# Half of the output projection's passes taken among the query products of the chunk ahead

## The chip, the cores and the metric

The kernel runs on one core of a Trainium2 chip. The metric is the time of one execution on the device in microseconds (us), of which lower is better. A core has five engines with a queue of instructions each, worked off in order: TensorE (PE in the profile; its weight loads are a row of their own, PEld), VectorE (DVE), ScalarE (ACT), GpSimd (POOL) and SyncE (SP), which here only issues DMA transfers. Engines wait for each other by semaphores.

## What is computed

One transformer layer on x of 2 x 1024 tokens x 512, all in f32: `x = x + layernorm(attention(layernorm(x)))`, then `x = x + layernorm(ffn(layernorm(x)))`. What matters here is the attention with its output projection, cut to its core:

```python
q = hidden_states @ Wq      # 32 heads of 128
k = hidden_states @ Wk      # 8 key heads, each for 4 query heads
v = hidden_states @ Wv
gs = log_sigmoid(k) / 16
o_lin = gla_scan(softmax(q), softmax(k), v, gs)      # S = S * exp(g_t) + k_t v_t;  o_t = q_t S
y = sliding_window_attn(rope(q), rope(k), v)         # window of 64
o_ = (0.5 * y + 0.5 * o_lin).astype(bfloat16).astype(float32)
o = o_ @ Wo                                          # 4096 -> 512
```

The feed-forward part first rounds its three weight matrices to 16 levels per block of 64 (NF4), and then computes `w3(silu(w1 x) * (w2 x))`.

## The kernel before, in words

The attention is `fast_attention`. Its main loop (`for n in range(N_)`, line 769) runs over 128 chunks in the order of key head g (8), batch b (2) and block of 128 tokens c (8). A chunk is the work of 128 tokens and the 4 query heads of one key head. Keys are made for two chunks at once, so even and odd iterations differ: an even one holds the key products of the next pair (`key_products`, line 412), an odd one holds the gates and the key transposes of that pair.

The loop is software-pipelined by hand. In iteration n the scores, the two attention parts and the values of chunk n are computed, the queries of chunk n + 1 are prepared, and the output of chunk n - 1 is projected. All engines are wrapped so that instructions keep the order in which the program writes them (`InOrder`, line 110; `product` is TensorE's matmul and records line 117, as every wrapped operation does). So the order on each engine is the order of calls in the loop body. On TensorE an odd iteration is:

- `scores(n)` (tile ps)
- `query_products(n + 1)` (tile pq): the 128 tokens times Wq for 4 heads, four products of 128x512 over the 512 inputs (kt = 0 to 3), two passes each in f32
- `key_gates` (pg), `linear(n)` (pa, and ot from the state S), `mix(n)` (softmaxed scores sw transposed into pa)
- `project(n - 1)` (tile py)
- `key_transposes` (pt, pg), `rope_transposes(n + 1)` (tr), `values(n)` (ot from A), `softmax_transposes(n + 1)` (tq), `state_products(n)` (pS)

In an even iteration `linear` follows the query products directly, then come `key_products` (pk) and `mix`, then `project`, `rope_transposes`, `softmax_transposes`, `values`.

What follows pq on the other engines: ScalarE copies it to q (line 509), GpSimd rotates q into qr by four operations (`rope`, line 377: qtmp, two halves of qr, their sum), and TensorE transposes qr (line 528), from which ScalarE copies qrT for the next scores. VectorE takes pq's maxima (nmq), ScalarE its exponentials in place, VectorE divides (qs), and TensorE transposes qs (tq).

What follows pk in even iterations: ScalarE copies it to kv, VectorE takes maxima (nmk), ScalarE makes gate and ke.

`project` (line 623) multiplies the rounded heads oc of chunk n - 1, 128x128 for each of 4 heads, by the head's rows of Wo. These stand in the tile wop as two parts, a rounded one and its remainder (i = 0, 1), both of type F32R; a product of F32R is one pass. So there are eight passes of 128x512 that add into one PSUM bank, py. The tile oc comes from ob by ScalarE: `heads(n)` scales ot into ob (bf16) at the end of iteration n, and `rounded_heads(n)` casts it to oc early in iteration n + 1. `collect` (line 631) adds py to yacc on VectorE. The tiles ot and py alternate in a pool of two PSUM banks (line 313), pq, pk and pg in another of two.

Between these calls, `signs` and `steps` place pieces of the weight rounding for the feed-forward part on ScalarE (zs, zp, zm) and VectorE. At the end of each key head the next Wo rows are split into wop by GpSimd (`part_weights`). The last 16 iterations also begin the feed-forward part.

Of the kernel before, what the change touches and what calls it, by code (L numbers as in the profile page):

```python
# [11 lines left out]
F32 = mybir.dt.float32  # L12
# [9 lines left out]
P = 128  # L22
NB, N, HID = 2, 1024, 512
H, KVH, D, W = 32, 8, 128, 64
GRP = H // KVH
# [95 lines left out]
def sandwich_kernel(ctx: ExitStack, tc: tile.TileContext, x, wq, wk, wv, wo, w1, w2, w3, out, con):  # L121
# [154 lines left out]
    def load_out_weights(g):  # L276
        nc.sync.dma_start(wos, wo[g * GRP * D : (g + 1) * GRP * D, :].rearrange("(h p) d -> p h d", p=P))
        return wos
# [20 lines left out]
    def fast_attention():  # L299

        with ExitStack() as attn:
# [11 lines left out]
            po = attn.enter_context(tc.tile_pool(name="fpo", bufs=2, space=PSUM))  # L313
# [3 lines left out]
            product = tensor.matmul  # L317
# [5 lines left out]
            def parts_tile(name):  # L323
                return wop.tile([P, 2, GRP, HID], F32R, tag="wop", name=name)
# [43 lines left out]
            weights = {0: (*first_weights, parts_tile("wop0"), load_out_weights(0))}  # L368
# [8 lines left out]
            def rope(dst, tmp, src, c, nch, heads):  # L377

                shape = [P, nch, heads, D]
                hd = D // 2  # L380
                cs = cosT[:, c : c + nch, :].unsqueeze(2).to_broadcast(shape)
                sn = sinT[:, c : c + nch, :].unsqueeze(2)
                gpsimd.tensor_tensor(tmp, src, cs, ALU.mult)
                half = [P, nch, heads, hd]
                gpsimd.tensor_tensor(dst[:, :, :, 0:hd], src[:, :, :, hd:D], sn[:, :, :, 0:hd].to_broadcast(half), ALU.mult)
                gpsimd.tensor_tensor(dst[:, :, :, hd:D], src[:, :, :, 0:hd], sn[:, :, :, hd:D].to_broadcast(half), ALU.mult)
                gpsimd.tensor_tensor(dst, dst, tmp, ALU.add)
# [20 lines left out]
            chunks = [(g, b, c) for g in range(KVH) for b in range(NB) for c in range(NCH)]  # L408
            N_ = len(chunks)
            keys, Q, S = {}, {}, {}  # L410
# [87 lines left out]
                gpsimd.memset(eq[:, :, W : W + 1], 1.0)  # L498
                K.update(krT=krT, khT=khT, khz=khz, eq=eq, em=em, before=None)

            def query_products(n):

                g, b, c = chunks[n]
                ci = b * NCH + c
                pq = pmm.tile([P, GRP, D], F32, tag="mm", name="pq")
                for kt in range(KT):
                    product(pq.rearrange("p h d -> p (h d)"), lhsT=xnT[:, kt, ci * P : (ci + 1) * P], rhs=weights[g][0][:, kt, :], start=kt == 0, stop=kt == KT - 1)
                q = q1p.tile([P, GRP, D], F32, tag="q", name="q")
                scalar.copy(q, pq)
                qr = q1p.tile([P, GRP, D], F32, tag="qr", name="qr")  # L510
                tmp = q1p.tile([P, GRP, D], F32, tag="qtmp", name="qtmp")
                rope(qr.unsqueeze(1), tmp.unsqueeze(1), q.unsqueeze(1), c, 1, GRP)
                Q[n] = {"pq": pq, "qr": qr}
# [55 lines left out]
            def score_masks(n):  # L569
                sc = Q[n]["sc"]  # L570
                vector.tensor_tensor(sc, sc, fwin[:, 1 if chunks[n][2] == 0 else 0], ALU.add)
                Q[n]["nms"] = row_max(sc, 4, "s")

            def score_exps(n):
                Q[n]["sms"] = row_exps(Q[n]["sc"], Q[n]["sc"], Q[n]["nms"], 4, "s")
# [42 lines left out]
            def rounded_heads(n):  # L618
                oc = q2p.tile([P, GRP, P], F32R, tag="oc", name="oc", bufs=1)
                scalar.copy(oc, Q[n]["ob"])  # L620
                Q[n]["oc"] = oc

            def project(n):
                g, oc, parts = chunks[n][0], Q[n]["oc"], weights[chunks[n][0]][2]
                py = po.tile([P, HID], F32, tag="o", name="py")
                for h in range(GRP):
                    for i in range(2):
                        product(py, lhsT=oc[:, h, :], rhs=parts[:, i, h, :], start=h == 0 and i == 0, stop=h == GRP - 1 and i == 1)
                Q[n]["py"] = py

            def collect(n):

# [136 lines left out]
            for n in range(N_):  # L769
                g, b, c = chunks[n]  # L770

                inputs = [AHEAD + n] if AHEAD + n < NCI else []
                even = n % CB == 0
                more, keys2 = n + 1 < N_, n + CB < N_


                scores(n)
                if n:
                    rounded_heads(n - 1)
                score_masks(n)  # L780
                query_decays(n)
                if n:
                    next_state(n - 1)
                if n == N_ - 2:
                    F.token_sums(0, vector)
                signs(2 if even else 1, n)
                steps(1, n)
                score_exps(n)
                if more:
                    query_products(n + 1)  # L790
                if even:
                    query_max(n + 1)
                    query_exps(n + 1)
                    signs(3, n)
                    score_softmax(n)
                    steps(1, n)
                    linear(n)
                    if keys2:
                        key_products(n + CB)
                    else:  # L800
                        first = F.hidden(0, 0, ("gate", "gate", "tr", "tr"))
                        next(first)
                    query_softmax(n + 1)
                    steps(1, n)
                    for ci in inputs:
                        input_norms(ci)
                        input_measured(ci + 1)
                    feed_forward_tokens(n)
                    if keys2:
                        key_softmax(n + CB)  # L810
                    mix(n)
                    steps(1, n)
                    if keys2:
                        key_sums(n + CB)
                    if n:
                        project(n - 1)
                        collect(n - 1)
                    if not keys2:
                        next(first)
                    rope_transposes(n + 1)  # L820
                    softmax_transposes(n + 1)
                    signs(1, n)
                    values(n)
                    heads(n)
                    steps(2, n)
                    if n == 0:
                        for h in range(2, GRP):
                            part_weights(0, h)
                else:
                    if not more:  # L830
                        for i in range(4):
                            next(first)
                    score_softmax(n)
                    if not more:
                        next(first)
                        next(first)
                        list(F.weight_sums(1))
                    if more:
                        query_max(n + 1)
                        key_gates(n + 1)  # L840
                        query_exps(n + 1)
                        key_decays(n + 1)
                    signs(2, n)
                    linear(n)
                    mix(n)
                    if more:
                        query_softmax(n + 1)
                    project(n - 1)
                    collect(n - 1)
                    for ci in inputs:  # L850
                        input_norms(ci)
                        input_measured(ci + 1)
                    feed_forward_tokens(n)
                    if more:
                        key_transposes(n + 1)
                        rope_transposes(n + 1)
                    else:
                        second = F.hidden(0, 1, ("gate", "gate", "up", "tr"))
                        for i in range(4):
                            next(second)  # L860
                    values(n)
                    if more:
                        softmax_transposes(n + 1)
                    heads(n)
                    steps(2, n)
                state_products(n)
                for ci in inputs:
                    input_transposes(ci)
                feed_forward_begun(n)
                if b == 1 and c == 0 and g + 1 < KVH:  # L870
                    weights[g + 1] = all_weights(g + 1)
                if b == 1 and NCH - GRP <= c and g + 1 < KVH:
                    part_weights(g + 1, c - NCH + GRP)
            rounded_heads(N_ - 1)
            for i in range(4):
                next(second)
            project(N_ - 1)
            collect(N_ - 1)
            list(F.weight_sums(2))

# [670 lines left out]
```

## Time and profile before

| | |
|---|---|
| median of 3 runs | 2108.78 us (2108.52 to 2109.44) |
| the profiled execution | 2109.49 us, of which the span from first to last instruction is 2107.6 us |
| granted TensorE clock, mean | 0.998 |
| DMA | 64.65 MB, 31 GB/s in the mean |

The profile's page lists, for each engine, busy time and its share of the span. Then it has rows of one form: line, engine, operation, output tile <- input tiles, sizes, count; behind the first bar are busy time and mean ns of one; behind the second the idle time of the engine before them and who ended it. A matmul's record contains the time until its results are drained, which overlaps the next matmul, so that spacing and duration differ. The timeline gives instructions in order of time: start in us, length in us (of several merged ones together), engine, line, operation, tiles, count, and in brackets the idle time before and who ended it. The chain that ended last is followed back from the end; its rows give start and length of each piece. The attention's loop fills the time from some 30 us to 1660 us; behind it stands the rest of the feed-forward part.

### The profile page before, as it was taken

What the parts mean: (1) busy time and instruction counts of PE and PEld (TensorE: products, weight loads), DVE (VectorE), ACT (ScalarE), POOL (GpSimd) and SP (SyncE); (2) the same over time, 40 slices, a digit from 0 to 9 for tenths busy, and PEclk for the clock granted to TensorE, in tenths of its full rate; (3) what the DMA queues carried; (4) which work ended last, traced back from release to release, by engine and by line L of the source; (5) the groups of instructions that cost most, each with busy time, mean ns of one, the idle gap of its engine ahead of it and who ended that gap; (6) DMA issues with size and microseconds to landing.
All of it is one profiled execution on the core that took longest, in us unless ns stands there. A gap on an engine that the chain in (4) does not pass through costs nothing.

```text
span 2107.6 us, 29467 instructions
## 1 busy us (share of the span) xinstructions
PE 2067.5 (98%) x9476; PEld 1503.0 (71%) x9476; DVE 1593.1 (76%) x3123; ACT 1394.4 (66%) x4045; POOL 1125.8 (53%) x1524
## 2 busy tenths in 40 slices
PE   7999999999999999999999999999999999999998
PEld 4767777777777777777777777777767785858583
DVE  4888888888888888888888888788886663838352
ACT  4777888888888888888888888888876440202010
POOL 5555755565566556554655574556554452627250
PEclk9999999999999999999999999999999999999999
DMA  6100100010011001000100010000011030000000
GB/s 226 36 11 20 57 16 11 21 51 10 11 36 40 11 16 41 31 11 11 50 21 10 26 57 12 11 17 22 16 36 35 26 102 21 21 20 16 21 1 22
DMA packets 48307, 64.65 MB, mean 31 GB/s; under 512 B 6736, under 2 KB 22736, under 8 KB 48144
## 3 DMA queue, kind: packets, MB, share of 16 engines
q1 hardware_dynamic: 48144, 62.68, 9.4%
q8 instruction: 77, 1.26, 0.2%
q14 instruction: 86, 0.70, 0.1%
HBM read 50.01 MB, written 12.65 MB: 30 GB/s over the span
## 4 chain that ended last, share of the span: by engine, by line
PE 82%; DVE 7%; ACT 6%; POOL 3%; issue 1%; DMA 0%; ACTq 0%; POOLq 0%; DVEq 0%
PE pq L117 17%; PE pout L117 12%; PE py L117 9%; PE pk L117 8%; PE ot L117 8%; PE pa L117 6%; PE ps L117 5%; PE pup L117 3%; PE pgate L117 3%; PE tr L117 3%; PE tq L117 2%; ACT ps L117 2%; PE pg L117 2%; POOL qr L117 1%; ACT pq L117 1%
## 5 line engine op out<-in xcount | busy, mean ns | idle before, releaser
L117 POOL TENSOR_TENSOR qtmp<-q,tables 128x512 f32<-128x512 f32 x128 | 162.5, 1270 | 568.4 <-ACT q L117 564.0
L117 PE MATMUL pq<-wq,xnT 128*128 128x512 f32 x1024 | 460.7, 592 | 1.6 <-ACT xnT L117 1.6
L117 PEld LDWEIGHTS pq<-wq,xnT 128*128 128x128 f32 x1024 | 184.8, 190 | 185.4 <-issue 185.4
L117 ACT ACTIVATE zs<-xw,fbounds 128x512 bf16<-128x512 f32 (+3 forms) x416 | 287.9, 723 | 0.0
L117 PE MATMUL py<-wop,oc 128*128 128x512 f32 x1024 | 270.8, 406 | 0.0
L117 ACT ACTIVATE ps<-ps,nms 128x128 f32<-128x128 f32 x512 | 175.1, 342 | 111.4 <-DVE nms L117 96.9
L117 ACT ACTIVATE pq<-pq,nmq 128x128 f32<-128x128 f32 x512 | 175.2, 342 | 91.7 <-DVE nmq L117 79.3
L117 PE MATMUL pk<-wkv,xnT 128*128 128x256 f32 x1024 | 231.5, 379 | 0.0
L117 PEld LDWEIGHTS pk<-wkv,xnT 128*128 128x128 f32 x1024 | 194.5, 190 | 46.5 <-issue 16.3
L117 PEld LDWEIGHTS py<-wop,oc 128*128 128x128 f32 x1024 | 182.9, 189 | 35.0
L117 POOL TENSOR_TENSOR qr<-q,tables 128x256 f32<-128x256 f32 x256 | 206.6, 828 | 0.0
L117 DVE SCALAR_TENSOR_TENSOR zp<-zp,zs 128x512 f32<-128x512 f32 (+3 forms) x224 | 196.9, 879 | 9.2 <-ACT zs L117 4.7
L117 POOL TENSOR_TENSOR qr<-qr,qtmp 128x512 f32<-128x512 f32 x128 | 165.8, 1295 | 10.1
L117 DVE SCALAR_TENSOR_TENSOR zm<-zm,zs 128x512 f32<-128x512 f32 (+3 forms) x192 | 163.6, 852 | 5.3 <-ACT zs L117 2.9
L117 DVE TENSOR_TENSOR ps<-ps,fwin 128x512 f32<-128x512 f32 x128 | 89.2, 697 | 101.9 <-PE ps L117 101.2
L117 PE MATMUL ps<-kT,qrT 128*128 128x128 f32 x1024 | 136.7, 277 | 2.8 <-POOL kT L117 2.6
L117 DVE TENSOR_REDUCE nmq<-pq 128x4 f32<-128x512 f32 x128 | 87.8, 686 | 62.2 <-ACT q L117 61.2
L117 POOL TENSOR_TENSOR rstd<-ve,mhalf 128x1 f32<-128x1 f32 x62 | 36.5, 588 | 172.3 <-DVE ve L117 172.2
L117 PEld LDWEIGHTS ps<-kT,qrT 128*128 128x128 f32 x1024 | 124.8, 192 | 5.0 <-POOL kT L117 4.0
L117 PE MATMUL ot<-qh,S 128*128 128x512 f32 x224 | 114.4, 592 | 0.0
L117 POOL COPY vm<-kv 64x128 f32<-64x128 f32 (+1 forms) x176 | 99.6, 581 | 3.1
L117 ACT ACTIVATION_READ_ACCUMULATOR pq<-pq,nmq 128x1 f32 x512 | 98.8, 193 | 0.0
(311 smaller groups left out, 4587.0 us busy)
## 6 DMA issues: line engine op xcount, KB each, us to landing
wq<-in_L_attn_Wq_dram SPq DMA_DIRECT2D x8, 1024.0 KB, 5.6
wos<-in_L_attn_Wo_dram SPq DMA_DIRECT2D x8, 1024.0 KB, 5.4
wq<-_attn_hidden_states_dram SPq DMA_DIRECT2D x20, 256.0 KB, 2.8
xw<-in_L_ffn_w_dram SPq DMA_DIRECT2D x20, 256.0 KB, 2.6
dq<-zp SPq DMA_DIRECT2D x20, 256.0 KB, 2.0
wos<-dq SPq DMA_DIRECT2D x20, 256.0 KB, 2.7
out_dram<-ffoc SPq DMA_DIRECT2D x16, 256.0 KB, 2.0
tokens<-_attn_hidden_states_dram SPq DMA_DIRECT2D x12, 256.0 KB, 5.4
```

Source lines behind the costliest of these rows:

```text
L117: return lambda *args, **kwargs: self.tc.keep_in_program_order(getattr(self.engine, name)(*args, **kwargs))
```

## The change

In every iteration but the first, the four passes of `project(n - 1)` with part i = 0 are called from within `query_products(n + 1)`, one behind each of its four products. The four with i = 1 stay at the place of the former call. The eight products and what they add up to are the same; their order goes from head outermost to part outermost. The tile py is opened with the first of them. In the last iteration, which has no query ahead, the first four are called where the query products would be, and the projection of the last chunk makes both calls one after the other. `skip_group_check` is an argument for the program's builder and no instruction.

```diff
-            def query_products(n):
+            def query_products(n, done=None):
...
                 for kt in range(KT):
                     product(pq.rearrange("p h d -> p (h d)"), lhsT=xnT[:, kt, ci * P : (ci + 1) * P], rhs=weights[g][0][:, kt, :], start=kt == 0, stop=kt == KT - 1)
+                    if done is not None:
+                        project(done, 0, [kt])
...
-            def project(n):
-                g, oc, parts = chunks[n][0], Q[n]["oc"], weights[chunks[n][0]][2]
-                py = po.tile([P, HID], F32, tag="o", name="py")
-                for h in range(GRP):
-                    for i in range(2):
-                        product(py, lhsT=oc[:, h, :], rhs=parts[:, i, h, :], start=h == 0 and i == 0, stop=h == GRP - 1 and i == 1)
-                Q[n]["py"] = py
+            def project(n, i, heads=range(GRP)):
+
+                oc, parts = Q[n]["oc"], weights[chunks[n][0]][2]
+                if "py" not in Q[n]:
+                    Q[n]["py"] = po.tile([P, HID], F32, tag="o", name="py")
+                for h in heads:
+                    product(Q[n]["py"], lhsT=oc[:, h, :], rhs=parts[:, i, h, :], start=i == 0 and h == 0, stop=i == 1 and h == GRP - 1, skip_group_check=True)
...
                 if more:
-                    query_products(n + 1)
+                    query_products(n + 1, n - 1 if n else None)
+                elif n:
+                    project(n - 1, 0)
...
-                        project(n - 1)
+                        project(n - 1, 1)
                         collect(n - 1)
...
-                    project(n - 1)
+                    project(n - 1, 1)
                     collect(n - 1)
...
-            project(N_ - 1)
+            project(N_ - 1, 0)
+            project(N_ - 1, 1)
             collect(N_ - 1)
```

## The prediction, made before the result was known

> **What bounds the kernel now.** I read the page first: its busy shares, then its rows for the two products that the change touches.
>
> ```profile
> PE 2067.5 (98%) x9476; PEld 1503.0 (71%) x9476; DVE 1593.1 (76%) x3123; ACT 1394.4 (66%) x4045; POOL 1125.8 (53%) x1524
> ...
> L117 PE MATMUL pq<-wq,xnT 128*128 128x512 f32 x1024 | 460.7, 592 | 1.6 <-ACT xnT L117 1.6
> ...
> L117 PE MATMUL py<-wop,oc 128*128 128x512 f32 x1024 | 270.8, 406 | 0.0
> ```
>
> TensorE is busy for 98% of the span and the granted clock stands at full speed in every slice. So the time is the sum of TensorE's passes plus the few holes between them. A mean of one (592, 406 ns) contains the drain of a pass that overlaps the next one, so it is no price. The price I take from the chain that ended last, in order of time, for the stretch 1000 to 1030 us. It holds one even iteration (n = 76) and one odd one (n = 77), and only TensorE stands in it:
>
> ```profile
> 1005.18 3.45 PE pk L117 x16
> ...
> 1009.07 1.88 PE py L117 x8
> ...
> 1013.80 3.44 PE pq L117 x8
> ...
> 1021.70 0.44 PE pt L117 x4
> 1022.13 0.22 PE pg L117 x2
> 1022.35 0.44 PE tr L117 x4
> ```
>
> A query product of one chunk is eight passes in 3.44 us (0.43 each), the output projection eight passes in 1.88 us (0.235 each). An odd iteration lasts 11.40 us and an even one 13.75. In this stretch TensorE never idles, so at first sight moving passes around inside one iteration costs and gives nothing. What matters is who else stands ready just in time. I therefore followed the query of the chunk ahead through the other engines, in the timeline of the odd iteration n = 77:
>
> ```profile
> 1013.64 3.60 PE L117 MATMUL pq<-wq,xnT 128*128 128x512 f32 x8
> ...
> 1022.19 0.60 PE L117 MATMUL tr<-ident,qr 128*128 128x128 f32 x4
> ...
> 1017.33 0.59 ACT L117 COPY q<-pq 128x512 f32<-128x512 f32 x1
> ...
> 1018.00 1.27 POOL L117 TENSOR_TENSOR qtmp<-q,tables 128x512 f32<-128x512 f32 x1 [1.77 <-ACT q L117]
> 1019.22 1.43 POOL L117 TENSOR_TENSOR qr<-q,tables 128x256 f32<-128x256 f32 x2
> 1020.73 1.29 POOL L117 TENSOR_TENSOR qr<-qr,qtmp 128x512 f32<-128x512 f32 x1
> ```
>
> The reader is to see a chain with no air in it. The last pass of pq ends at 1017.24 (13.64 + 3.60). ScalarE's copy starts 0.09 us later, GpSimd had idled 1.77 us for that copy, and its four rope operations end at 1022.02. TensorE's transposes of qr are recorded at 1022.19. I read the same two records in all 62 odd iterations from n = 3 to 125: from the end of qr to the first transpose it is 0.10 us in the median and never under 0.05. The 0.05 is the price of the signal itself. So the true slack is 0.05 us. In even iterations, which have the key products between, the same distance is 2.05 in the median and at least 1.03. The list of what waits on the tile qr says the same: the weight loads of these transposes already wait for it now and then.
>
> ```profile
>   PEld tr L117: 7.6, 22
> ```
>
> **The change part by part.** Per chunk the projection still has eight products with as many weight loads; there is no DMA in them and nothing is added on SP's or any other queue. Four of the eight move from behind the softmaxed scores' transposes to among the query products: one behind each pair of pq passes.
>
> *The price of a moved pass.* In a block it takes 0.233 us start to start; at the edges against an f32 pass the records give about 0.240. A moved pass stands alone between f32 passes, so 0.240 is its nearest row. Bounds: 0.216 if the surplus over a plain stream came from py following py, 0.245 if both edges are paid. Here a rule of the Trainium skill speaks. "TensorE: Matmul & The Clock Gate", section "Back-to-back issue gap", prices a warm pass of N columns at N/2.4 + 2.5 ns, 216 ns for 512, and its Part 2 says that weight loads are pulled ahead under a running matmul. By that a pass between long f32 passes could be 19 ns cheaper than the 235 of the chain. But the trace has the py weight loads (0.19 us) already under the pass before, each issued at its start, so there is no load left to hide, and the pass is 0.233 all the same. By the rule three moved passes delay pq by 0.65, by the row by 0.72. I take the row. The four moved passes then cost 4 x 0.005 = 0.02 us more per chunk; over 64 even iterations that is 1.3 us (in odd ones it disappears in the wait below). By the rule it would be a gain of 4.7 us in the even iterations.
>
> *The delay of pq.* Three of the four moved passes stand ahead of pq's last pair. pq therefore ends 3 x 0.24 = 0.72 us later. On ScalarE the copy q waits at the head; behind it are ex and the decay exps and the query exps, which have over 0.8 us to spare before TensorE asks for their results. On GpSimd the rope follows the copy directly. TensorE meanwhile reaches the transposes of qr at the same time as before, since four passes less stand in the later block. So in an odd iteration it now waits 0.72 - 0.05 = 0.67 us there, and behind it in its queue are the values' products, the softmax transposes, the state product and the next scores. Nothing fills that hole, TensorE having no slack to catch up with. 63 odd iterations have a query ahead: 63 x 0.67 = 42.2 us. In even iterations 2.05 us of slack swallow the delay: 0. If the pass is at its bounds, it is 63 x 0.60 = 37.8 or 63 x 0.69 = 43.5.
>
> *The key products.* In even iterations pk stands behind pq and ends 4 x 0.24 = 0.96 us later, and ScalarE is waiting for it:
>
> ```profile
> 1008.67 0.59 ACT L117 COPY kv<-pk 128x512 f32<-128x512 f32 x1 [0.62 <-PE pk L117]
> ...
> 1012.73 0.60 ACT L117 ACTIVATE ob<-ot 128x512 bf16<-128x512 f32 x1
> ...
> 1013.36 0.62 ACT L117 CAST oc<-ob 128x512 fp32r<-128x512 bf16 x1
> ```
>
> Behind kv stand the gates, ke, qrT, a sign, ob and oc, and oc is what the first moved pass of the next (odd) iteration needs; behind that pass stand the other pq passes and all of the iteration. In a typical even iteration this chain has 0.25 us of air before qrT (which waits for tr), 0.21 before ob (which waits for ot), and oc is ready 0.53 before its new slot, of which 0.05 is the signal: 0.94 in sum against 0.96. qrT to the next scores: 0.25 + 0.69 = 0.94. So typically 0.02 us are missing; in about one even iteration of three ScalarE is late already or has a second sign there, and 0.2 to 0.5 are missing. I take 0.1 on average, 63 x 0.1 = 6.3 us; bounds 0 and 0.4 (25 us).
>
> *The later masks.* The transposes of sw into pa also come 0.96 us later, and with them VectorE's A, which the values' products need. From A's end to those products it is 2.07 us in odd iterations and 1.30 in typical even ones, so 0.3 is left: 0. In nine even iterations near the two ends TensorE waits for A already, by VectorE's own load; I leave these as they are.
>
> *The longer life of py.* Its PSUM bank is opened some 4 to 8 us earlier. The bank's last reader, the sum into yacc of the iteration before, ends at 1012.40, and the first moved pass comes at 1014.50: 2.1 us of cover, so 0 (without cover the first pass would wait as long as the sum is late). oc is overwritten only after the second half, as now. The other order of the eight products changes no count: 0. The last iteration and the tail only split the block: 0.
>
> Sum: 42.2 + 6.3 + 1.3 = 49.8 us on top of the profiled execution's 2109.49 (span 2107.6), which lies 0.7 above the median of the runs, 2108.78. So 2108.78 + 49.8 = 2158.6; I say 2158.
>
> **The rivals.** *Faster, at about 2099.* The py passes, set between passes of twice their length, drop to 216 ns: 127 x 4 x 0.019 = 9.6 us less. That requires that the transposes of qr not wait. It decides at the delay of pq: under 0.05 us nothing waits, and each 0.1 us above costs 6.3 us, so the gain is gone at 0.2 us of delay. For it: TensorE is at 98%, a cheaper pass is real time. Against it: the 4.78 us from the end of pq to the end of qr (0.09 + 0.59 + 0.08 + 4.02) hold only work and signals. 5%.
>
> *ScalarE sets the pace, about 2183.* If the even iterations' chain from pk to oc misses 0.5 us and not 0.1 (0.96 of delay with half of the air gone, as in the iterations where ScalarE is late already), it is 63 x (0.67 + 0.5) + 1.3 = 75 us. For it: ScalarE is at eight tenths in slices 4 to 26. Against: the typical iteration has the 0.94. 12%.
>
> *Only the rope waits, with cheap passes, about 2142.* 63 x 0.60 - 4.7 = 33 us, nothing from ScalarE. 20%.
>
> *The change does nothing, within 4 us of before.* It would take an engine order in which the rope starts before pq ends, which the tile-wide copy excludes; or two effects cancel. 3%.
>
> **How the numbers follow.** The likeliest case (rope waits, ScalarE a little) has 60%; its own range is 2148 to 2172. With the two rivals on its side the range is 2134 to 2182. Something under a fifth stays outside, the fast case included. A change under 0.2% (4 us) can't be told from none by the runs. Faster 5%, same 3%, slower 92%.
>
> **What the profile of the changed kernel would show.** TensorE's idle before tr, released by POOL qr, rises from 2.3 us in 8 times to some 40 us in about 60, all in odd iterations; odd iterations last about 12.1 us and even ones about 13.8. pq's eight passes and the first three moved ones end 0.7 us later after their start. In the rows, tr's idle is the largest on TensorE, with a smaller one before py by ACT oc or before ps by ACT qrT. What would make me wrong: moved passes at other than 0.24 us, seen in py's start to start; a copy q that begins at the old time; or GpSimd's rope running shorter.

## The result and the profile after

The changed kernel takes 2168.05 us in the median of 5 runs (2167.65 to 2170.27), the kernel before 2108.78: a ratio of 1.0282, with a 95% interval of 1.0271 to 1.0293. It is 59 us slower; 50 were forecast. The profiled execution has a span of 2166.0 us at a granted clock of 0.997.

The page first. TensorE's share fell by a point. The query products, among which the passes were moved, idle no more than before (1.6 us); py waits 2.8 us where it waited for nothing. The idle time that matters stands at the transposes of qr, in the list of waits below.

```profile
PE 2091.4 (97%) x9476; PEld 1504.9 (69%) x9476; DVE 1588.7 (73%) x3123; ACT 1398.0 (65%) x4045; POOL 1129.6 (52%) x1524
...
PE 66%; ACT 11%; POOL 11%; DVE 9%; issue 2%; DMA 0%; ACTq 0%; POOLq 0%; DVEq 0%
...
L117 PE MATMUL py<-wop,oc 128*128 128x512 f32 x1024 | 541.2, 590 | 2.8 <-ACT oc L117 2.8
L117 PE MATMUL pq<-wq,xnT 128*128 128x512 f32 x1024 | 522.2, 592 | 1.6 <-ACT xnT L117 1.6
```

The second line is the engines' share of the chain that ended last. TensorE held 82% of it before; now GpSimd and ScalarE have 11% each, after 3% and 6%. That py's busy time seems to double (270.8 to 541.2) is a trap: the record of most moved passes now begins while the pq pass ahead is still running. TensorE did the same passes in the same time, as the chain shows below.

TensorE's waits, longest in total first, name the new one (us in total, times, longest):

```profile
PE tr L117 <- POOL qr L117: 29.2, 63, 0.8
PE ot L117 <- DVE A L117: 12.1, 12, 2.2
...
PE py L117 <- ACT oc L117: 2.8, 8, 0.5
```

Before, the first stood at 2.3 us in 8 times and the second at 5.5 in 6. There are 63 odd iterations with a query ahead, and every one waits. The chain of the odd iteration n = 77 shows how (start, length), and behind it stands the row of tr from the timeline:

```profile
1048.60 0.86 PE pq L117 x2
1049.46 0.24 PE py L117
1049.70 0.86 PE pq L117 x2
1050.56 0.23 PE py L117
1050.79 0.86 PE pq L117 x2
1051.65 0.24 PE py L117
1051.89 0.87 PE pq L117 x2
...
1052.84 0.59 ACT q L117
1053.43 0.07 issue
1053.50 1.27 POOL qtmp L117
1054.77 1.40 POOL qr L117 x2
1056.17 0.07 issue
1056.24 1.29 POOL qr L117
1057.53 0.04 issue
1057.57 0.66 PE tr L117 x4
...
1057.57 0.66 PE L117 MATMUL tr<-ident,qr 128*128 128x128 f32 x4 [0.41 <-POOL qr L117]
```

A moved pass takes 0.23 to 0.24 us: no dearer than in a block, and no cheaper. From the end of pq (1052.76) the chain leaves TensorE for 4.8 us. TensorE had done its own work by then and stood idle before tr. The list of waits shows less than the loss, because a record of these transposes lasts 0.27 us while they start 0.11 us apart: the first 0.16 us of a hole lie under the drain of the record before it. That makes 29.2 + 63 x 0.16 = 39 us, against 2.3 + 8 x 0.16 = 4 before. So by this estimate some 36 us are lost at tr.

Start to start of the scores, all odd iterations together last 44.3 us longer than before and all even ones 14.6. Below, every run is split in this way. Of the 44.3, 5.0 are lost before the first pq pass and 5.2 more by the time TensorE reaches pt; the rest is lost at tr.

### The profile page after: what moved, and what is told of

It reads as the page before. It is cut to its first block, busy times and chain, and to the rows that moved or that the text cites. A ratio compares the mean times of both kernels' runs of the same rounds, so it can differ in the third digit from the quotient of the medians.

```text
span 2166.0 us, 29582 instructions
## 1 busy us (share of the span) xinstructions
PE 2091.4 (97%) x9476; PEld 1504.9 (69%) x9476; DVE 1588.7 (73%) x3123; ACT 1398.0 (65%) x4045; POOL 1129.6 (52%) x1524
## 4 chain that ended last, share of the span: by engine, by line
PE 66%; ACT 11%; POOL 11%; DVE 9%; issue 2%; DMA 0%; ACTq 0%; POOLq 0%; DVEq 0%
PE pq L117 18%; PE pout L117 11%; POOL qr L117 7%; PE pk L117 6%; PE py L117 5%; PE ot L117 5%; PE ps L117 5%; POOL qtmp L117 3%; PE pup L117 3%; PE pgate L117 3%; ACT q L117 2%; PE tr L117 2%; PE pa L117 2%; ACT pq L117 2%; PE tq L117 2%
## 5 line engine op out<-in xcount | busy, mean ns | idle before, releaser
L117 PE MATMUL py<-wop,oc 128*128 128x512 f32 x1024 | 541.2, 590 | 2.8 <-ACT oc L117 2.8
L117 PE MATMUL pq<-wq,xnT 128*128 128x512 f32 x1024 | 522.2, 592 | 1.6 <-ACT xnT L117 1.6
L117 PE MATMUL ps<-kT,qrT 128*128 128x128 f32 x1024 | 141.6, 281 | 3.3 <-POOL kT L117 1.9
L117 ACT COPY q<-pq 128x512 f32<-128x512 f32 x128 | 74.9, 585 | 72.5 <-PE pq L117 72.3
L117 PE MATMUL tr<-ident,qr 128*128 128x128 f32 x512 | 80.8, 281 | 29.3 <-POOL qr L117 29.2
```

The lines of the kernel that those rows point to most:

```text
L117: return lambda *args, **kwargs: self.tc.keep_in_program_order(getattr(self.engine, name)(*args, **kwargs))
```

## The experiments

Times are medians with their ratio to the kernel before, run on the same chip (2108.8 to 2109.8 there). "Odd" and "even" are the changes of these iterations' sums against the profiled kernel before.

| run | us | ratio (95% interval) | odd | even |
|---|---|---|---|---|
| the change | 2168.05 | 1.0282 (1.0271 to 1.0293) | +44.3 | +14.6 |
| block of four behind pq | 2131.18 | 1.0101 (1.0084 to 1.0118) | +21.5 | +1.7 |
| even iterations only | 2145.12 | 1.0170 (1.0153 to 1.0187) | +21.4 | +14.5 |
| odd iterations only | 2145.70 | 1.0171 (1.0154 to 1.0188) | +35.9 | 0.0 |
| the change, short rope | 2128.37 | 1.0087 (1.0070 to 1.0104) | +11.3 | +7.8 |
| odd only, block behind pq | 2111.06 | 1.0009 (1.0003 to 1.0016) | +1.9 | +1.6 |
| odd only, one pass ahead | 2119.61 | 1.0050 (1.0033 to 1.0067) | +9.9 | +1.6 |
| block behind pq, key sums later | 2129.05 | 1.0095 (1.0078 to 1.0111) | +20.2 | +0.4 |
| block behind pq, a step earlier | 2130.56 | 1.0104 (1.0088 to 1.0119) | +6.4 | +15.5 |
| the change, tr later | 2155.02 | 1.0219 (1.0202 to 1.0236) | +26.7 | +20.0 |
| before, part outermost | 2109.59 | 1.0000 (0.9992 to 1.0009) | +0.2 | +1.3 |
| before, norms behind A | 2102.74 | 0.9969 (0.9957 to 0.9981) | +2.5 | -8.1 |
| the change, norms behind A | 2158.00 | 1.0227 (1.0210 to 1.0244) | +48.7 | +0.4 |

**Is it the delay of pq?** The theory: three moved passes delay the end of pq, and through the copy q and the rope the transposes of qr. Two rivals: what stands behind all four passes is what costs (A), or the moved passes themselves are dearer (B). Four runs, the first with the moved passes in one block behind the whole of pq:

```diff
-                        project(done, 0, [kt])
+                        project(done, 0, ([], [], [], range(GRP))[kt])
```

> The four moved passes stand in one block behind the whole of pq, so pq is not delayed, while everything behind it (key products, gates, pa) comes as late as in the changed kernel. Theory (pq's delay by three passes, carried through q and the rope to TensorE's wait at tr in odd iterations, is most of the loss): the wait at tr goes back to 2 to 4 us in all, and the time to about 2117 us (2110 to 2125), the rest being key products that still come 0.93 us later. Rival A (what stands behind all four passes, pk above all, is what costs): 2155 us or more. Rival B (an F32R pass alone between f32 passes costs TensorE 0.1 us more each): 2109, with pq and py spaced as before.

It came out at 2131: most of the loss goes, but 21.5 us stay where 8 were expected, nearly all in odd iterations. The wait at tr is 9.6 us in 30 times, where 2 to 4 us were expected.

```diff
-                    query_products(n + 1, n - 1 if n else None)
+                    query_products(n + 1, n - 1 if n and n % CB == 0 else None)
```

(The odd half has `== 1` in place of `== 0`; in both, the other parity keeps all eight in the old place, by a second change that is not shown.)

> Only even iterations take four passes among the query products; odd ones keep all eight in the old place, part outermost. Theory: even iterations have 2 us of slack at tr, so only what the changed kernel lost in even iterations and its share at the next scores remains, 10 to 20 us: about 2124 us. Rival A: the key products stand in even iterations alone, so nearly all of the loss stays, 2155 us or more. Rival B: half the moved passes, half the loss, 2138 us.

> Only odd iterations take four passes among the query products. Theory: 63 times 0.65 us at tr, some 41 to 44 us: 2150 to 2153 us. Rival A: no key products behind, so 2115 us or less. Rival B: 2138 us.

The odd half costs 35.9 us, all of it in odd iterations, and its trace has the same wait at tr (29.0 us, 63 times). But the even half costs as much, where 10 to 20 us were expected, and 21.4 us of it stand in odd iterations in which nothing was moved. The two together make 72, more than the change's 59, so they partly hide each other. Neither the theory nor a rival had said that.

The fourth leaves out the rope's last sum on the queries, so their cosine term is missing (`add` is False for the queries, True for the keys; the call is not shown).

```diff
-                gpsimd.tensor_tensor(dst, dst, tmp, ALU.add)
+                if add:
+                    gpsimd.tensor_tensor(dst, dst, tmp, ALU.add)
```

> The changed kernel without the last of the rope's four operations on the queries (the sum of the two terms, 1.29 us of GpSimd per chunk), so the queries' rotation lacks its cosine term; all passes stay where the change puts them. Theory: GpSimd has qr ready 1.29 us earlier, more than the 0.65 us that TensorE waits, so the wait at tr is gone in odd iterations and 40 of the 59 us come back: about 2127 us (2120 to 2135). Rival A and rival B: nothing on TensorE changes and the chain behind pk stays, so 2160 to 2168 us.

2128: with the rope 1.29 us shorter the wait at tr is gone from the list, and 40 us come back. Rivals A and B, for which the rope is nothing, are out for this part.

**The dose, in odd iterations alone.** The odd half again, with a table of heads as above: one pass ahead of pq's last pair (`[], [], [0], [1, 2, 3]`) or none.

> Only odd iterations move four passes, and in one block behind the whole of pq: no delay of pq, and no key products behind it. Theory (in odd iterations only the delay of pq counts, through q and the rope): as before, within 3 us of 2109. Rival A (what stands behind the moved passes, here pg, pa and sw's transposes, carries loss as well): 2118 us or more. Rival B (a switch of type costs TensorE): as before too, since the block has the two edges that it had.

> Only odd iterations; one moved pass ahead of pq's last pair, three behind. Theory: the delay is one pass, 0.233 us, less the 0.05 of slack at tr, 0.18 to 0.24 us in each of 63 odd iterations: 2120 to 2124 us. With three passes ahead (odd iterations only) it was 36 us. Rival B: one moved pass alone and a block of three, about 0.1 us in each, 2115 us.

None ahead: 1.8 us. One: 10.3. Three: 36. The delay is priced: in the median odd iteration it is 0.18 us for one pass of 0.23 and 0.635 for three (0.70), so 0.05 to 0.06 us of slack, as forecast. The mean is lower (9.9 / 63 = 0.16 and 35.9 / 63 = 0.57), since some iterations have more slack. What stands behind the passes in odd iterations costs next to nothing: 1.8 us, with an interval of 0.6 to 3.4.

**What did the even half do to odd iterations?** With the block behind pq the key products come 0.93 us late in even iterations. In the next odd iteration the copy q starts 0.38 us behind the end of pq in the median (0.09 before), with ScalarE busy up to it. Its timeline there, in n = 77, and pq's row on TensorE:

```profile
1031.59 0.19 ACT L117 ACTIVATION_READ_ACCUMULATOR ps<-ps,nms 128x1 f32 x1
1031.68 0.57 ACT L117 COPY q<-pq 128x512 f32<-128x512 f32 x1
...
1027.71 3.60 PE L117 MATMUL pq<-wq,xnT 128*128 128x512 f32 x8
```

pq ends at 1031.31, but the copy stands behind the score exponentials. Those wait for the scores' maxima, and these for the mask, on VectorE. Its timeline in the same run, with the scores on TensorE:

```profile
1024.20 0.42 DVE L117 TENSOR_REDUCE nmk<-pk 128x2 f32<-128x256 f32 x1 [0.52 <-ACT kv L117]
1024.54 0.68 DVE L117 TENSOR_TENSOR A<-pa,fcausal 128x512 f32<-128x512 f32 x1
...
1026.22 0.17 DVE L117 RECIPROCAL rsk<-smk 128x2 f32<-128x2 f32 x1 [0.27 <-ACT ke L117]
1026.30 0.67 DVE L117 TENSOR_TENSOR yacc<-yacc,py 128x512 f32<-128x512 f32 x1
1026.89 1.53 DVE L117 SCALAR_TENSOR_TENSOR zm<-zm,zs 128x512 f32<-128x512 f32 x2
1028.34 0.69 DVE L117 TENSOR_TENSOR ps<-ps,fwin 128x512 f32<-128x512 f32 x1
...
1026.72 1.16 PE L117 MATMUL ps<-kT,qrT 128*128 128x128 f32 x8
```

The scores are ready at 1027.88, the mask starts 0.46 us later and has no wait in its brackets: VectorE was still at the work that began late with kv. Before, in the same iteration, the scores were ready at 1013.81 and the mask followed at once:

```profile
1013.84 0.70 DVE L117 TENSOR_TENSOR ps<-ps,fwin 128x512 f32<-128x512 f32 x1
...
1012.75 1.06 PE L117 MATMUL ps<-kT,qrT 128*128 128x128 f32 x8
```

So the second theory is a chain over two iterations: late pk, kv, the keys' maxima, A and the rest on VectorE, the mask, the score exponentials, q, the rope, tr. Two runs tested it. First, VectorE's wait for ke was taken off it, by moving the keys' reciprocal to the next odd iteration:

```diff
-                    if keys2:
-                        key_sums(n + CB)
...
                     if more:
+                        key_sums(n + 1)
                         query_max(n + 1)
```

> As the run with all four passes in a block behind pq (21.5 us over before), and the keys' reciprocal, for which VectorE waits on ScalarE's ke in even iterations, is taken in the next odd iteration, ahead of the query maxima. Second theory (the late key products hold VectorE at that reciprocal; so yacc, the rounding steps and the next scores' mask and maxima come late, with them ScalarE's score exponentials and the copy q behind them, and TensorE waits at tr in the odd iteration): the wait for ke, 0.3 us in a typical even iteration, leaves the path, and half or more of the 21.5 us comes back: 2112 to 2120 us. Rival (ScalarE itself is late, by its own work between kv and the exponentials): within 3 us of 2131.

2129, a miss, and the time that the rival had named: the mask stood where it was, 0.48 us behind the scores in both runs in the median. The wait of 0.27 was gone, but the rounding step behind yacc, which began 0.4 us earlier, became longer (1.15 for 0.73 us in the median). In n = 76 the two steps behind yacc take 1.95 us in place of 1.53:

```profile
1024.92 1.95 DVE L117 SCALAR_TENSOR_TENSOR zm<-zm,zs 128x512 f32<-128x512 f32 x2
1026.80 0.69 DVE L117 TENSOR_TENSOR ps<-ps,fwin 128x512 f32<-128x512 f32 x1
...
1025.16 1.16 PE L117 MATMUL ps<-kT,qrT 128*128 128x128 f32 x8
```

So this run couldn't tell. Second, one of the two rounding steps at the end of an even iteration was taken earlier, where VectorE waits for kv:

```diff
                     query_softmax(n + 1)
-                    steps(1, n)
+                    steps(2, n)
...
                     heads(n)
-                    steps(2, n)
+                    steps(1, n)
```

> As the run with four passes in one block behind pq (21.5 us over before), and one of the two rounding steps that end an even iteration on VectorE is taken earlier, between the softmax of the queries and the maxima of the keys, where VectorE idles about 0.7 us for kv. Theory (the late key products push the keys' maxima, A and the work behind them on VectorE, without a hole, into the next scores' mask; the copy q waits behind the score exponentials): the mask comes up to 0.45 us earlier in odd iterations, q is again set by pq, and most of the loss in odd iterations is gone: 2112 to 2120 us. Rival (it is ScalarE's own work, kv to oc, that is late): within 3 us of 2131.

The time missed: 2130.56 is what the rival had named. But the trace shows the mechanism of the theory. VectorE in the same iteration, with the scores' row:

```profile
1025.38 0.69 DVE L117 SCALAR_TENSOR_TENSOR zm<-zm,zs 128x512 f32<-128x512 f32 x1 [0.35 <-ACT zs L117]
1025.99 0.69 DVE L117 TENSOR_TENSOR ps<-ps,fwin 128x512 f32<-128x512 f32 x1
...
1024.78 1.16 PE L117 MATMUL ps<-kT,qrT 128*128 128x128 f32 x8
```

The mask again follows the scores (1025.94) at once, q follows pq, and the odd iterations' loss falls from 21.5 to 6.4 us. But the earlier step now delays A in the even iterations where VectorE is full: TensorE's wait for A rose from 5.5 to 13.8 us, and the even iterations lose 15.5. The gain was given back at the next wait. Of the 6.4 us that odd iterations still lose, 5.8 arise ahead of the first pq pass, at the scores, which start 0.05 us behind the end of qrT in the median as they do in the change.

**Is the loss a matter of tr's place?** The change with tr behind the values' products in odd iterations:

```diff
                         key_transposes(n + 1)
-                        rope_transposes(n + 1)
...
                     values(n)
                     if more:
+                        rope_transposes(n + 1)
                         softmax_transposes(n + 1)
```

> The changed kernel with the transposes of qr in odd iterations taken behind the values' products (0.86 us of TensorE's work) in place of ahead of them. Theory: TensorE does those 0.86 us while the rope ends 0.65 us late, so the wait at tr is gone; qrT comes up to 0.2 us later than the next scores want it, which may be given back: 2168 less 63 times 0.45 to 0.68, about 2130 us (2125 to 2142). Rival A and rival B: the loss is not at tr, 2160 us or more.

2155: 13 us come back, not 38. TensorE's wait for qr is gone, but a new one took its place:

```profile
PE ps L117 <- ACT qrT L117: 4.2, 13, 0.3
```

Most of these holes lie under the drain; in the median odd iteration the next scores are recorded 0.145 us behind the end of qrT and still come 0.38 us later than before. The query's chain from pq over q, the rope, tr and qrT to the scores has little air in sum, wherever tr stands.

**Controls, and the even iterations.** The order alone, all eight in the old place:

```diff
-                for h in range(GRP):
-                    for i in range(2):
+                for i in range(2):
+                    for h in range(GRP):
```

> The kernel before with only the order of the eight passes changed, part outermost as in the change, all in the old place. Theory: no cost in the order, each pass loads its weights anyway: within 2 us of before. Rival: the same weights twice in a row are cheaper, so up to 0.02 us for each of 1024 passes: 2115 to 2130 us.

Nothing, 2109.59. Last, TensorE's wait for A. In the first and the last few even iterations VectorE normalises rows ahead of the keys' maxima and A. They were moved behind them, in the kernel before and in the changed one:

```diff
-                    for ci in inputs:
-                        input_norms(ci)
-                        input_measured(ci + 1)
-                    feed_forward_tokens(n)
                     if keys2:
                         key_softmax(n + CB)
                     mix(n)
+                    for ci in inputs:
+                        input_norms(ci)
+                        input_measured(ci + 1)
+                    feed_forward_tokens(n)
```

> The kernel before, with the norms of input rows and of the feed-forward's tokens that VectorE takes in some even iterations moved from ahead of the keys' maxima and A to behind them. TensorE waits 5.5 us in all for A in those iterations (12.1 us in the changed kernel). If these norms are what makes A late there, that wait goes and the time is 2103 to 2107 us; if the work merely moves to the next wait, as before.

> The changed kernel with the same move of the norms behind A. In the changed kernel TensorE waits 12.1 us for A against 5.5 before; in the loaded even iterations (the first and the last few) it lost 0.7 us each. If the delayed query maxima reach A through these norms, the move takes back the 5.5 and most of the 6.6 us: 2168 less 9 to 14, 2154 to 2159 us. Rival (A is late there by the query's own chain of maxima, exponentials and quotient, norms or not): only what the kernel before gained, 2161 us or more.

The kernel before gains 6.8 us (ratio 0.9969, interval 0.9957 to 0.9981) and beats both. The changed one gains 10, and its wait for A falls from 12.1 to 2.6 us. So some 3 us of the change's loss came through these norms.

The rest of the even iterations' loss is there in the even-only run (14.5 us) and absent with the block behind pq (1.7), so it comes from the delay of pq and not of pk. The traces show the way. The maxima nmq on VectorE start with the copy q, 0.70 us later in the median. In n = 48, before and after, with the start of the values' products (the scores start at 648.68 and 670.25):

```profile
653.88 0.69 DVE L117 TENSOR_REDUCE nmq<-pq 128x4 f32<-128x512 f32 x1 [1.49 <-ACT q L117]
...
659.22 0.68 DVE L117 TENSOR_TENSOR A<-pa,fcausal 128x512 f32<-128x512 f32 x1
...
660.51 0.60 PE L117 MATMUL ot<-A,vm 128*128 128x256 f32 x2
```

```profile
676.16 0.69 DVE L117 TENSOR_REDUCE nmq<-pq 128x4 f32<-128x512 f32 x1 [2.19 <-ACT q L117]
...
681.50 0.68 DVE L117 TENSOR_TENSOR A<-pa,fcausal 128x512 f32<-128x512 f32 x1
...
682.23 0.70 PE L117 MATMUL ot<-A,vm 128*128 128x256 f32 x2
```

Between nmq and A VectorE has no hole over 0.15 us in either kernel, so A ends 0.70 us later. It ended 0.61 us ahead of the products that need it; now it ends 0.05 ahead, and they wait for it. This iteration loses 0.50 us, half of it here and half at the next scores, which now start 0.05 us behind the end of qrT. In all 26 even iterations that lose over 0.1 us, A ends 0.55 to 0.71 us later. Nine of them had no air at A before (0.05 to 0.06 us) and lose 7.4 us together. Ten more, each the first of its block of eight chunks, had 0.30 to 0.61 and lose 5.4; such a chunk has no product with the state S, so TensorE comes to A earlier.

## Why the prediction was right, point by point

*The price of a moved pass* (0.24 by the row, 0.216 by the rule that the Trainium skill's "TensorE: Matmul & The Clock Gate" gives under "Back-to-back issue gap"): the row was right, 0.23 to 0.24, and no run here shows 0.216. The rival of cheaper passes is out. The gain that the rule would have given doesn't exist, and the 1.3 us charged for edges don't either: in even iterations TensorE reaches tr 1.3 us earlier in sum, not later.

*The delay of pq* (42.2 us at tr in odd iterations): right in place and count, a little large in size. 63 of 63 iterations wait there. The median iteration is as forecast (0.635 us for 0.67), but moving the passes in odd iterations alone costs 35.9 us, since some have more slack. That odd iterations lost 44.3 in the change is near 42.2 by the next term's help.

*The key products* (6.3 us, by way of qrT and oc): near in size, and the ways named are the ones that the trace shows. Odd iterations lose 8.4 us more in the change than in the odd half alone, and 8.2 of these are there before TensorE reaches pt, ahead of the wait at tr. 5.0 arise at the scores: in even iterations qrT ends 0.06 us ahead of the next scores in the median, 0.74 before, and these take longer. Around n = 76, before and after:

```profile
1011.51 0.58 ACT L117 COPY qrT<-tr 128x512 f32<-128x512 f32 x1
...
1012.75 1.06 PE L117 MATMUL ps<-kT,qrT 128*128 128x128 f32 x8
```

```profile
1046.81 0.58 ACT L117 COPY qrT<-tr 128x512 f32<-128x512 f32 x1
...
1047.44 1.16 PE L117 MATMUL ps<-kT,qrT 128*128 128x128 f32 x8
```

The other 3.2 arise among the moved passes, which wait for oc. The 0.1 us booked for each iteration was a guess at a mean over unlike iterations, so that it came so near is in part luck. What the prediction did not see is a third way: the late pk delays VectorE, and through the next scores' mask the copy q, which is the larger part of the 21.5 us that the block behind pq costs. In the change that way is covered by the delay of pq, since q waits for the later of the two: in the median odd iteration the exponentials end 5.06 us after the scores' start and pq at 5.30, and q starts 0.09 us behind pq, as before.

*"In even iterations 2.05 us of slack swallow the delay: 0"*: right for tr, where nothing waits in even iterations. But the delay of pq has a second way, over nmq and VectorE to A, and the prediction followed pq to ScalarE and GpSimd only.

*The later masks* (A: "0.3 is left: 0"): this is the step that was mis-sized. A was to come 0.96 us later by way of sw, with 1.30 us of air in typical even iterations, and nine near the two ends in which TensorE waits for A already were left "as they are". Where it mattered A came 0.70 later by way of nmq. Where a wait has no air, any delay of it counts in full: the nine without air (n = 56 and 104 among them, in the middle) lost 7.4 us, and ten with 0.30 to 0.61 of air lost 5.4. Even iterations lost 14.6 us in all against the 1.3 booked for them.

*The life of py, the order of the products*: 0, as said; the run with the order alone has 2109.59.

The sum thus came to 49.8 for 59.3: in odd iterations 48.5 for 44.3, in even ones 1.3 for 14.6. The way through tr, most of the loss, was right; the total is nearer than its parts, since the two errors have opposite signs, and that much is luck.

## What to carry to other kernels

An engine that is busy 98% of the time can still hang on a chain that is just in time: look at the gap between each result's end and its consumer's start, and ask which of them is only the signal's own 0.05 us. Follow a delayed result to every reader, and look at the iterations with the least air, not at the typical one. Here passes put ahead of a product cost TensorE itself nothing and the chain behind that product 36 us; put behind it, in the iterations that hold no key products, they cost 1.8. Delays that meet at one wait took the larger here, not the sum, so each half of the change cost more than half of it, and a repair of one may show nothing until the other is gone.

## What the runs showed of the hardware

F32R passes set singly between f32 passes run at the pace that they have in a block (0.23 to 0.24 us for 128x512), and the order of the passes makes no difference (2109.59 us for 2109.5). After the 63 holes before tr TensorE's first transpose takes 0.17 us to the next, not 0.11. A wait of up to 0.16 us leaves no gap in TensorE's rows, since a record of 0.27 us stands for a transpose that is followed 0.11 us later. And one step of VectorE took 1.15 us in place of 0.73 when it began 0.4 us earlier, while GpSimd was at the keys' rope; no run isolates the cause.
